# Three groups of blocks instead of two in a fused RWKV layer with routed experts

## The chip, the cores and the metric

The kernel runs on one core of one Trainium2 chip. The metric is the device time of one execution in microseconds; less is better. The core has five engines, each with its own queue of instructions that it works through in order: TensorE (PE in the profile, its weight loads PEld), VectorE (DVE), ScalarE (ACT), GpSimd (POOL) and SyncE (SP, which here only issues DMAs). They meet through semaphores. DMAs are issued from SP, from ACT at the start, and from GpSimd where the addresses come from data.

## The reference

The input is `x`, 8 sequences of 1024 tokens with 256 features, all float32. Two layers follow each other, each with a residual:

```
x = x + rwkv(layernorm(x))           # time mix, then channel mix, each with its own layernorm inside
x = x + experts(layernorm(x))

# time mix: r, w, k, v = projections 256 -> 256
e = exp(w + k), w = -exp(...)
num = decay * num + e * v ; den = decay * den + e     # along the 1024 tokens
x = x + Wo(sigmoid(r) * num / den)
# channel mix: 256 -> 1024 -> 256
x = x + sigmoid(Wrec xn) * Wval(relu(Wkey xn) ** 2)

# experts, 32 of them, 256 -> 128 -> 256
gates = sigmoid(xt @ expert_sel.T)
sel_val, sel_idx = top_k(gates, 4)
out = sum over the 4 chosen e of sel_val_e * relu(xt @ keys[e]) @ values[e]
```

The 8192 tokens make 32,768 pairs of token and expert.

## The kernel before

**Blocks.** The tokens are cut into 16 blocks of 512 (`TB`). `period(i)` (L943) emits in one pass the dense work of several blocks that are at different places: the channel mix of block `i` (`channel`, eight slices of 128 of the 1024 inner features), the time mix of block `i + 1` (`mix_wk`, `mix_vr`, `mix_scan`, `mix_out`), the first norms of block `i + 2`, and the routing of block `i - 1` (`norm_d` to `gates_by_row`). `total_blocks + 1` periods are emitted, and the last one holds only the routing of block 15. The result of the channel mix goes to DRAM as `acc` (`channel_end`, L424), the start value for the later sums.

**Scatter.** `gates_of` finds the four chosen experts of each token, and `rows_of` (L482) gives each pair a row in a DRAM buffer `xs` that has one region per expert. A region has place for all the tokens of a group and for one tile more. `scatter` (L527) queues 16 indirect DMAs per block, one for 128 tokens and one of the four choices; `post` (L543) issues them from GpSimd, two per `advance`. Each row carries its token's features and 8 tags, by which its place in the result is found again. `clear` (L170) fills the front of each region beforehand, so that rows which no token takes are told by their tag.

**Groups.** `GROUPS = (11, 5)`: blocks 0 to 10 are group 0, blocks 11 to 15 group 1. Each group has its own `xs`, and its own `ys` for the experts' results. When a group's blocks are all scattered, `tile_table` (L571) works out on VectorE, from the group's counts, which expert and which rows each tile of 256 (`TS`) rows has. A group has `tokens * 4 / 256 + 16` tiles, since the rows of an expert seldom fill a whole tile: 88 + 16 = 104 and 40 + 16 = 56. The last 16 tiles of a group have two halves with different experts.

**Experts.** `experts(g, pause)` (L687) is a generator that emits one step per tile. A step fetches a tile two steps ahead (`fetch`, SP), transposes one (`turn`, TensorE; `trx`), copies the key weights of its expert (`keys`, VectorE, 315 ns a copy), multiplies an earlier one with the keys (`hidden`; `ph`), and a still earlier one with the values (`result`; `po`, L800). ACT copies the result to `yg` (L865), and `send` (L810) issues two indirect DMAs from GpSimd that write the rows to their places in `ys` (L812); rows without a token have a place out of bounds and are not written. `places` (L740) works out these places as `to`. There are three `yg` buffers and six `to` buffers, and each comes free when the sends that read it have landed.

**Sums.** `combine(g)` (L869) is a generator too. A part of it has 128 tokens: a load of their four result rows each (`g`, 512 KB, L887) and four additions on VectorE (`ac`, L894), each a multiplication by the gate and an addition. Four parts make a block, whose start value is loaded from `acc` and whose sum is stored to `out`. A load from `ys` has to wait until all sends of the group have landed. Group 0 has 44 parts, group 1 has 20.

**What sets the order.** The list `background` holds generators with a rate. `advance` (L919), of which a period has 16, posts two scatters and lets each generator take as many steps as its rate says. `beside` adds a generator, and `drain` advances until the list is empty. The order of emission is:

```
    for i in range(total_blocks + 1):
        if i == len(groups[0]) + 1:
            post(len(waiting))
            beside(experts(0, 4), 113 / (STEPS * 3))
        if i == total_blocks - 1:
            drain()
            beside(combine(0), 0.5)
        period(i)
        ...
    post(len(waiting))
    beside(experts(1, 0), 1)
    drain()
    beside(combine(1), 1)
    drain()
```

So group 0's tiles lie in periods 12 to 14, its sums begin in period 15 and go on beside group 1's tiles, and group 1's sums stand alone at the end. A scheduler then orders the instructions of each engine; the tiles keep their order (`pinned`).

Of the kernel before, what the change touches and what calls it, by code (L numbers as in the profile page):

```python
# [8 lines left out]
F32 = mybir.dt.float32  # L9
# [4 lines left out]
ALU = mybir.AluOpType  # L14
# [5 lines left out]
P = 128  # L20
# [5 lines left out]
NOWHERE = float(1 << 20)  # L26
RUN = 8
TS = 256
GROUPS = (11, 5)


@with_exitstack
def rwkv_then_routed_experts(
# [18 lines left out]
    nc = tc.nc  # L52
    B, S, D = x.shape
    F = w_key.shape[-1]
    NE = w_exp.shape[1]
# [78 lines left out]
    region1, xs, ys, n_tiles, regions = [], [], [], [], []  # L134
    for g, members in enumerate(groups):
        gt = len(members) * TB
        r = const.tile([P, NT, NE], F32, name=f"region1_{g}")
        nc.gpsimd.iota(
            r,
            pattern=[[0, NT], [gt + TS, NE]],  # L140
            base=TS + 1,
            channel_multiplier=0,
            allow_small_or_imprecise_dtypes=True,
        )
# [24 lines left out]

    def clear(g):  # L170

        zeros = p3.tile([P, DX], F32, tag="k2", name=f"zeros_{g}")
        nc.gpsimd.memset(zeros, 0.0)
        nc.gpsimd.memset(zeros[:, D : D + 1], NOWHERE)
        front_rows = xs[g][: regions[g], :].rearrange("(e r) d -> e r d", e=NE)[:, :TS, :]
        fills = []
        for j in range(SJ):
            fills.append(
                nc.sync.dma_start(
                    out=front_rows[:, j * P : (j + 1) * P, :].rearrange("e p d -> p e d"),  # L180
                    in_=zeros[:, None, :].to_broadcast([P, NE, DX]),
                )
            )
# [118 lines left out]
    def mix_scan(i, c):  # L302
        n = blocks[i][1]
        m = mine[i]
        ek, ev, rc, tail = m["ek", c], m["ev", c], m["rw"][:, c, :], m["tail"]
        last = mine[i - 1]["tail"] if n else None
        num0 = last[:, 0, c : c + 1] if n else 0.0
        den0 = last[:, 1, c : c + 1] if n else 0.0
        decay = edec[:, c : c + 1].to_broadcast([P, TB])
        nc.vector.tensor_tensor_scan(ek, decay, ek, den0, ALU.mult, ALU.add)  # L310
        nc.vector.tensor_tensor_scan(ev, decay, ev, num0, ALU.mult, ALU.add)
        if n + 1 < NB:
            nc.gpsimd.tensor_copy(tail[:, 0, c : c + 1], ev[:, TB - 1 : TB])
# [168 lines left out]
    def rows_of(i):  # L482
# [18 lines left out]
            nc.tensor.matmul(ps, ones, prior, start=False, stop=True, skip_group_check=True)  # L501

        key = p2.tile([P, NT, NE], F32, tag="key", name=f"key_{i}")
        nc.vector.tensor_tensor(key, ps, region1[g], ALU.add)
        nc.vector.tensor_tensor(key, key, chosen, ALU.mult)
        k8 = p2.tile([P, NT, 8], F32, tag="k8", name=f"k8_{i}")
        for t in range(NT):
# [50 lines left out]
    def gates_by_row(i):  # L558
# [9 lines left out]
            nc.vector.tensor_reduce(gate[:, :, k], eq, AX.X, ALU.add)  # L568
        routed[i] = gate

    def tile_table(g):  # L571


# [23 lines left out]
        up = small([NE], "up", I32)  # L597
        nc.vector.tensor_scalar(up, ps, float(H - 1), None, ALU.add)
        base = small([NE], "base")
        nc.vector.tensor_tensor(base, ps, region1[g][:, 0, :], ALU.add)  # L600
# [42 lines left out]
        for k in range(3):  # L643
# [21 lines left out]
        nc.vector.scalar_tensor_tensor(  # L665
            say, whole, live[:, 0:1], say, ALU.mult, ALU.add
        )


        stride = len(groups[g]) * TB + TS  # L670
# [9 lines left out]
        nc.tensor.transpose(ps, say.rearrange("p a b -> p (a b)"), ident)  # L680
        table = keep.tile([4, P], I32, name=f"table_{g}")
        nc.vector.tensor_copy(table, ps)
        return table, limit

    WHY = "made from counts that sum to the group's choices"

    def experts(g, pause):  # L687

        table, limit = tile_table(g)
        T = n_tiles[g]  # L690
        yield

        EXPERT, ROW = range(0, 4, 2)
        most = {EXPERT: NE - 1, ROW: regions[g]}
# [140 lines left out]
        for step in range(-FETCH, T + 2 * STAGE):  # L835
# [16 lines left out]
            if step < T:  # L852
                xgT = turned[step] = p3.tile([P, KC, TS], F32, tag="xgT", name=f"xgT_{g}_{step}")

                move = nc.scalar.copy if g == len(groups) - 1 else nc.vector.tensor_copy
                after(move(xgT, trx), signal)  # L856
                to[step] = places(step, xg)
            if step < T:
# [73 lines left out]
    def drain():  # L932
        while background:
            advance()

    def beside(stream, rate):
        background.append([stream, rate, 0.0])

    def do(piece, i, *args):
# [77 lines left out]
    mix_vr(1, 1)  # L1017
    apply_c(0)
    mix_scan(1, 0)
    for i in range(total_blocks + 1):  # L1020
        if i == len(groups[0]) + 1:
            post(len(waiting))
            beside(experts(0, 4), 113 / (STEPS * 3))
        if i == total_blocks - 1:
            drain()
            beside(combine(0), 0.5)
        period(i)
        if i == 0:
            clear(1)
        if 1 <= i < 5:  # L1030
            load_experts(i - 1)
    post(len(waiting))
    beside(experts(1, 0), 1)
    drain()
    beside(combine(1), 1)
    drain()


# [42 lines left out]
```

## Time and profile before

| | us |
|---|---|
| median of the runs (3) | 1632.53 |
| lowest and highest | 1628.62, 1640.68 |
| the profiled execution, its time | 1447.24 |
| its span | 1445.5 |

The profiled execution is quicker than the runs. Its mean granted TensorE clock was 0.948 of full speed. The page gives for its engines:

| engine | busy us | share |
|---|---|---|
| PE | 1253.0 | 87% |
| PEld | 883.6 | 61% |
| DVE | 982.9 | 68% |
| ACT | 554.6 | 38% |
| POOL | 646.2 | 45% |

In the profile, a line such as `L812 POOL DMA_INDIRECT ys<-yg,to` names the source line, the engine, the operation, and what is written from what. In a timeline the first two numbers are the start and the duration in us; what stands in brackets at the end is the time that the engine was idle before and what ended it ("issue" means that nothing which the profile shows was waited for). A row of a table of windows has the window, its length, busy time and number of instructions for PE, PEld, DVE, ACT and POOL, then the mean granted clock of TensorE, the share of time that the DMA engines were busy, and GB/s. For DMAs issued by GpSimd, the duration on POOL is not the time to landing.

### The profile page before, as it was taken

How to read it: one execution, taken by the hardware profiler on the slowest of the kernel's cores; microseconds unless marked ns; L12 is line 12 of the kernel's file. 1: busy time of each engine (PE TensorE's matmuls, PEld its weight loads, DVE VectorE, ACT ScalarE, POOL GpSimd, SP SyncE). 2: the span in 40 equal slices, each digit the busy share in tenths (PEclk: the TensorE clock that was granted, in tenths of full speed). 3: DMA queues.
4: the chain of work that ended last, by engine and by line, in shares of the span. 5: the costliest groups of instructions: out<-in, count | busy, mean ns of one | idle time of the engine just before them, and what ended most of it. 6: DMA issues, size and time to landing. Idle time of an engine off the chain costs nothing. (4 is left out here: it accounts for less than half of the span.)

```text
span 1445.5 us, 18879 instructions
## 1 busy us (share of the span) xinstructions
PE 1253.0 (87%) x5332; PEld 883.6 (61%) x5332; DVE 982.9 (68%) x3336; ACT 554.6 (38%) x1066; POOL 646.2 (45%) x653
## 2 busy tenths in 40 slices
PE   5899999999999999999889999999998752888730
PEld 2566666666566666666568767877787531666630
DVE  5757787787797797797758656765675375464528
ACT  3343543543543533534423443344332420444410
POOL 2112352351441441442436765776577344667640
PEclk9999999999999999999999999999999875999975
DMA  9244331421210210211234654555443486989748
GB/s 325 69 158 129 137 109 47 140 98 58 83 68 30 82 64 34 82 60 38 92 117 135 191 165 132 156 182 170 129 155 113 140 292 199 292 317 304 246 167 298
DMA packets 119415, 209.75 MB, mean 145 GB/s; under 512 B 17137, under 2 KB 77570, under 8 KB 118800
## 3 DMA queue, kind: packets, MB, share of 16 engines
q1 hardware_dynamic: 89616, 138.71, 31.1%
q0 software_dynamic: 27648, 68.23, 12.7%
q10 hardware_dynamic: 2048, 1.61, 0.3%
q8 instruction: 44, 0.72, 0.2%
q14 instruction: 59, 0.48, 0.1%
HBM read 105.68 MB, written 111.17 MB: 150 GB/s over the span
## 5 line engine op out<-in xcount | busy, mean ns | idle before, releaser
L812 POOL DMA_INDIRECT ys<-yg,to x320 | 324.3, 1013 | 212.2 <-ACT yg L865 129.4
L548 POOL DMA_INDIRECT xs<-x,row x256 | 254.7, 995 | 318.4 <-issue 291.6
L242 PE MATMUL pj_f<-xT,wkey 128*128 128x512 f32 x512 | 242.6, 596 | 0.0
L410 PE MATMUL cm<-wval,k 128*128 128x256 f32 x1024 | 240.0, 379 | 0.0
L410 PEld LDWEIGHTS cm<-wval,k 128*128 128x128 f32 x1024 | 194.3, 190 | 73.2 <-issue 52.1
L784 PE MATMUL ph<-xgT,key 128*128 128x256 f32 (+1 forms) x768 | 172.7, 355 | 37.3 <-DVE key L763 24.1
L402 ACT ACTIVATE k<-pj_f 128x512 f32<-128x512 f32 x128 | 76.4, 597 | 251.7 <-PE pj_f L242 251.7
L784 PEld LDWEIGHTS ph<-xgT,key 128*128 128x128 f32 x768 | 131.5, 195 | 64.8 <-issue 38.8
L800 PE MATMUL po<-wexp,hs 128*128 x640 | 167.8, 386 | 0.6 <-issue 0.6
L894 DVE SCALAR_TENSOR_TENSOR ac<-g,gate,ac 128x256 f32<-128x256 f32 x256 | 120.3, 482 | 68.9 <-DMA g<-ys 64.9
L862 ACT ACTIVATE hs<-ph 128x256 f32<-128x256 f32 x160 | 61.7, 386 | 193.9 <-PE trx L772 186.8
L242 PEld LDWEIGHTS pj_f<-xT,wkey 128*128 128x128 f32 x512 | 92.6, 190 | 65.1 <-issue 61.7
L856 DVE COPY xgT<-trx 128x512 f32<-128x512 f32 x104 | 71.0, 682 | 83.5 <-PE trx L772 83.3
L772 PE MATMUL trx<-ident,xg 128*128 128x128 f32 x640 | 100.0, 280 | 29.1 <-DMA xg<-xs 28.5
L800 PEld LDWEIGHTS po<-wexp,hs 128*128 128x128 f32 x640 | 113.8, 194 | 16.4 <-issue 6.2
L772 PEld LDWEIGHTS trx<-ident,xg 128*128 128x128 f32 x640 | 79.9, 144 | 47.5 <-DMA xg<-xs 17.3
L318 DVE RECIPROCAL rw<-rw 128x512 f32<-128x512 f32 x32 | 106.6, 3332 | 0.6
L865 ACT COPY yg<-po 128x512 f32<-128x512 f32 x160 | 93.5, 584 | 20.8 <-DMA ys<-yg,to 20.6
L403 ACT ACTIVATE k<-k 128x512 f32<-128x512 f32 x128 | 80.6, 630 | 4.0
L754 DVE TENSOR_TENSOR to<-order,xg 128x2 uint32<-128x2 f32 x160 | 25.9, 162 | 77.0 <-DMA ys<-yg,to 74.0
L856 ACT COPY xgT<-trx 128x512 f32<-128x512 f32 x56 | 32.8, 585 | 113.6 <-PE trx L772 112.8
L297 DVE TENSOR_TENSOR ev<-pj_v,ek 128x512 f32<-128x512 f32 x32 | 22.1, 691 | 75.9 <-PE pj_v L242 75.0
(173 smaller groups left out, 1827.4 us busy)
## 6 DMA issues: line engine op xcount, KB each, us to landing
xg<-xs SPq DMA_DIRECT2D x128, 264.0 KB, 3.0
g<-ys SPq DMA_DIRECT2D x64, 512.0 KB, 5.4
xs<-zeros SPq DMA_DIRECT2D x4, 4224.0 KB, 17.1
xg<-xs SPq DMA_DIRECT2D x64, 132.0 KB, 2.5
x<-in_x SPq DMA_DIRECT2D x16, 512.0 KB, 3.8
acc<-x SPq DMA_DIRECT2D x16, 512.0 KB, 2.9
wexp<-in_w_exp SPq DMA_DIRECT2D x4, 2048.0 KB, 11.0
ac<-acc SPq DMA_DIRECT2D x16, 512.0 KB, 5.5
```

The lines of the kernel that those rows point to most:

```text
L242: nc.tensor.matmul(ps, w(c), rhs[:, c, :], start=(c == 0), stop=(c == KC - 1))
L318: nc.vector.reciprocal(rc, rc)
L403: nc.scalar.activation(k2, k2, AF.Square)
L410: nc.tensor.matmul(m["cm"][t // 2][:, t % 2, :], k2[:, t * P : (t + 1) * P], wval[:, f, :], start=(f == 0 and t % 2 == 0), stop=(f == FC - 1),
L548: s = nc.gpsimd.indirect_dma_start(out=xs[g], out_offset=bass.IndirectOffsetOnAxis(ap=m["row"][:, t, k : k + 1], axis=0), in_=m["x3"][:, t ...
L772: nc.tensor.transpose(ps[:, c, j * P : (j + 1) * P], xg[:, j, c * P : (c + 1) * P], ident)
L784: nc.tensor.matmul(ps[:, cols], key[:, c * P : (c + 1) * P], xgT[:, c, cols], start=(c == 0), stop=(c == KC - 1),)
L800: nc.tensor.matmul(ps[:, j, :], hs[:, j * P : (j + 1) * P], wexp[:, bass.ds(e, 1), KC * P :], start=True, stop=True,)
L812: s = nc.gpsimd.indirect_dma_start(out=ys[g], out_offset=bass.IndirectOffsetOnAxis(ap=to[:, j : j + 1], axis=0), in_=yg[:, j, :], in_offse ...
L856: after(move(xgT, trx), signal)
L865: after(nc.scalar.copy(yg, po), signal)
L894: nc.vector.scalar_tensor_tensor(ac, gk, routed[i][:, t, k : k + 1], ac, ALU.mult, ALU.add)
```

## The change

`GROUPS` becomes (10, 5, 1): blocks 0 to 9, 10 to 14, and block 15 alone. The groups have 80 + 16 = 96, 40 + 16 = 56 and 8 + 16 = 24 tiles, 176 in all instead of 160, and 40, 20 and 4 parts of sums.

- Group 0's tiles start one period earlier, in period 11, and its sums in period 14.
- Group 1's tiles start in period 16, beside the routing of block 15.
- `tile_table` becomes a generator with one `yield`, behind the work on VectorE and ahead of the matmuls that turn the table round. `beside` takes the first step of a generator at once, so the first half is emitted then. `run` lets some steps pass between the halves (6 for group 0, 4 for group 1); for group 2 two advances lie between.
- Group 1's sums get the rate 0.7 and are put beside group 2's tiles (rate 1). Group 2's four parts stand alone at the end, with the more numerous load buffers that the last group had before.
- Group 1 and group 2 both let ACT copy the transposed tiles.
- `region1` no longer holds four equal copies, and the addition reads it by a broadcast. `clear` takes its zeros from another pool, and is called for the three groups in a row. The experts' weights are loaded one block later.

```
-GROUPS = (11, 5)
+GROUPS = (10, 5, 1)
...
-        r = const.tile([P, NT, NE], F32, name=f"region1_{g}")
+        r = const.tile([P, NE], F32, name=f"region1_{g}")
...
-        zeros = p3.tile([P, DX], F32, tag="k2", name=f"zeros_{g}")
+        zeros = p2.tile([P, DX], F32, tag="g", name=f"zeros_{g}")
...
-        nc.vector.tensor_tensor(key, ps, region1[g], ALU.add)
+        nc.vector.tensor_tensor(key, ps, region1[g][:, None, :].to_broadcast([P, NT, NE]), ALU.add)
...
     def tile_table(g):
...
+        yield
         stride = len(groups[g]) * TB + TS
...
-        return table, limit
+        tables[g] = table, limit
...
     def experts(g, pause):
-        table, limit = tile_table(g)
+        table, limit = tables[g]
         T = n_tiles[g]
-        yield
...
-                move = nc.scalar.copy if g == len(groups) - 1 else nc.vector.tensor_copy
+                move = nc.scalar.copy if g else nc.vector.tensor_copy
...
     def beside(stream, rate):
+        next(stream)
         background.append([stream, rate, 0.0])
...
+    def run(g, wait, pause):
+        making = tile_table(g)
+        next(making)
+        for _ in range(wait):
+            yield
+        for _ in making:
+            pass
+        yield from experts(g, pause)
+
     for i in range(total_blocks + 1):
-        if i == len(groups[0]) + 1:
+        if i == groups[0][-1] + 2:
             post(len(waiting))
-            beside(experts(0, 4), 113 / (STEPS * 3))
-        if i == total_blocks - 1:
+            beside(run(0, 6, 4), (n_tiles[0] + 9) / (STEPS * 3))
+        if i == groups[0][-1] + 5:
             drain()
             beside(combine(0), 0.5)
+        if i == groups[1][-1] + 2:
+            post(len(waiting))
+            beside(run(1, 4, 0), 1.6)
         period(i)
-        if i == 0:
-            clear(1)
-        if 1 <= i < 5:
-            load_experts(i - 1)
+        if i < 2:
+            clear(i + 1)
+        elif i < 6:
+            load_experts(i - 2)
     post(len(waiting))
-    beside(experts(1, 0), 1)
+    making = tile_table(2)
+    next(making)
+    for _ in range(2):
+        advance()
+    for _ in making:
+        pass
     drain()
-    beside(combine(1), 1)
+    beside(combine(1), 0.7)
+    beside(experts(2, 0), 1)
+    drain()
+    beside(combine(2), 1)
     drain()
```

More of the change, by code (lines that the diff above doesn't have):

```diff
@@ L136, in rwkv_then_routed_experts @@
         gt = len(members) * TB
-        r = const.tile([P, NT, NE], F32, name=f"region1_{g}")
+        r = const.tile([P, NE], F32, name=f"region1_{g}")
         nc.gpsimd.iota(
             r,
-            pattern=[[0, NT], [gt + TS, NE]],
+            pattern=[[gt + TS, NE]],
             base=TS + 1,
@@ L569, in gates_by_row @@
         routed[i] = gate
+    tables = {}
     def tile_table(g):
@@ L599, in tile_table @@
         base = small([NE], "base")
-        nc.vector.tensor_tensor(base, ps, region1[g][:, 0, :], ALU.add)
+        nc.vector.tensor_tensor(base, ps, region1[g], ALU.add)
         fh_i = small([2, NE], "fhi", I32)
```

## The prediction

> **What bounds the kernel now.** I read the slices of the page first, then windows, the timeline around the stage borders, and the chain. All times are of the profiled execution, 1447.2 us (span 1445.5 us plus 1.7 us around it).
>
> From the page, the slices (36 us each):
>
> ```profile
> PE   5899999999999999999889999999998752888730
> ...
> POOL 2112352351441441442436765776577344667640
> PEclk9999999999999999999999999999999875999975
> ```
>
> TensorE is full until about 1110 us, dips, and is not full again. GpSimd fills up exactly where tiles run.
>
> Windows of engine time (PE, weight loads, DVE, ACT, POOL with counts; then clock, DMA share, GB/s): a plain block; three blocks beside group 0's tiles; from the last block's store to the first send of group 1; the tiles of group 1; the end.
>
> ```profile
> 647.00:702.00 55.00, 54.13 (x205) 34.87 (x205) 43.48 (x146) 24.20 (x45) 21.11 (x22) 1.00 0.17 60
> 702.00:1095.00 393.00, 373.53 (x1794) 291.55 (x1795) 253.12 (x922) 151.19 (x315) 239.52 (x238) 0.98 0.49 150
> 1176.00:1232.00 56.00, 17.25 (x80) 13.52 (x81) 34.04 (x161) 7.69 (x16) 20.21 (x21) 0.57 0.69 227
> 1232.00:1380.00 148.00, 118.80 (x654) 96.32 (x652) 77.78 (x310) 68.71 (x150) 103.22 (x101) 0.99 0.87 287
> 1398.00:1446.00 48.00, 0.00 (x0) 0.00 (x0) 35.94 (x80) 0.00 (x0) 0.28 (x1) 0.50 0.82 297
> ```
>
> The first two rows are TensorE-bound. In the third TensorE works 17 of 56 us, in the last not at all. The fourth looks unsaturated on every engine, but the timeline of GpSimd shows that a send of 0.98 us is followed by 0.30 us without another reason:
>
> ```profile
> 1215.55 0.96 POOL L548 DMA_INDIRECT xs<-x,row  x1 [0.30 <-issue]
> 1231.74 1.11 POOL L812 DMA_INDIRECT ys<-yg,to  x1 [15.23 <-ACT yg L865]
> ...
> 1380.03 0.98 POOL L812 DMA_INDIRECT ys<-yg,to  x1 [0.30 <-issue]
> ...
> 1397.29 0.98 POOL L812 DMA_INDIRECT ys<-yg,to  x1 [0.30 <-issue]
> ```
>
> So a send cannot come faster than every 1.29 us, two per tile, 2.58 us. Over the 104 intervals from 1231.74 to 1380.03 one took 1.426 us: GpSimd is 90% taken, and the rest is waiting for `yg`. The chain's largest item is the same place, the landing of a send that frees a `yg` or `to` buffer:
>
> ```profile
> DMA ys<-yg,to 5%; DVE ac L894 2%; POOL ys L812 2%; DMA g<-ys 2%; DVE key L763 0%; DMA xg<-xs 0%; DVE to L754 0%; PE ph L784 0%; DVE order L752 0%; POOL xs L548 0%; DVE later L744 0%; DVEq L703 0%; POOLq L1077 0%; POOLq L812 0%; PE trx L772 0%
> ```
>
> TensorE's timeline gives its price of a tile beside blocks, and the stall of the table:
>
> ```profile
> 705.63 0.18 PE L596 MATMUL count<-total,ones 128*128 128x32 bf16 x1
> 711.68 0.39 PE L675 MATMUL all<-scratch,ones 128*128 128x256 bf16 x1 [5.87 <-DVE scratch L674]
> ...
> 764.25 1.03 PE L800 MATMUL po<-wexp,hs 128*128 x4
> 765.11 1.03 PE L784 MATMUL ph<-xgT,key 128*128 128x256 f32 x4
> 765.98 0.60 PE L772 MATMUL trx<-ident,xg 128*128 128x128 f32 x4
> 766.41 1.03 PE L800 MATMUL po<-wexp,hs 128*128 x4
> ```
>
> One tile is 766.41 - 764.25 = 2.16 us of TensorE.
>
> **What the Trainium skill says.** *Perfetto Trace Analysis*, DMA Instruction - SWDGE: for a DMA issued by GpSimd the profiled end is the end of descriptor generation, not of the movement. The trace agrees: a send shows 1013 ns, yet the chain holds a separate "DMA ys" item after it. *DMA: Bandwidth & Descriptors*, Anatomy of one DMA: about 2 us of such a DMA are fixed, mostly the write receipt. The trace's shortest is 2.4 us (last send 1397.29, next load 1399.71), and up to 6.8 us when DMA is busy. *TensorE: Matmul & The Clock Gate*, What's actually happening: after a few idle microseconds TensorE drops to half clock. The trace agrees: 0.50 in the last window. The same page, Architectural detail, says that ACT and DVE are strict first-in first-out; so a sum waiting for its load holds the tile operations behind it.
>
> **The change, part by part** (instructions counted in the order in which the changed program issues them).
>
> (a) *Fewer tiles beside blocks.* Group 0 has 80 + 16 = 96 tiles, not 104. 8 x 2.16 = -17.3 us, all TensorE-bound. The table's first half is now several advances ahead of its matmuls, so the 5.87 us stall goes: -5.9 us; bounds -5.9 and 0; what is late next there is nothing, TensorE has block work queued. But 13 tiles, not 10, are left after the last block's matmuls; uncovered they go at 2.74 us (10 in the 27.4 us from 1094.9 to 1122.3): 3 x 0.58 = +1.7. Sum -21.5.
>
> (b) *Sums beside block 14.* 10 parts of sums enter a block period. DVE there has 43.5 of 55 us taken; 10 parts x 4 additions x about 0.44 us (39 in 17.27 us at the end of the trace) = 18 us, less the 6 us of norms that no block 16 needs: 55 us, just TensorE's time. The period after it has DVE work of about 20 + 11 x 1.76 = 39 us against 35 of TensorE. +1, bounds 0 and +6. The 8 us in which TensorE waits behind ACT's `yg` copies at the end of group 0 (1122.3 to 1130.3) only move from block 15 to block 14.
>
> (c) *The gap before group 1.* From the store of the last block (1176.1) to the first send are 55.6 us: norms, gates, 16 scatters of block 15, then table and first tile. Group 1 now needs block 14, whose scatters end 5 us after that store (1181.1 against 1176.1). The first fetch came 1.6 us after the last scatter, the first send 13.6 us after that fetch: 20.2. The table needs 7.5 us of DVE after the store, with a few sums between; On SP one load of sums stands ahead of that fetch, and its buffer is free by then. I take 24, bounds 20 and 30. -31.6.
>
> (d) *The send stage.* It grows from 112 sends to 160 (56 + 24 tiles) plus the 16 scatters of block 15, now in the same queue of GpSimd, ahead of sends 8 to 18 of group 1; who waits for that is `yg`, then ACT, then TensorE. 159 intervals x 1.426 = 226.7; 16 x 1.27 (scatter and gap) = 20.3; where scatters stand GpSimd does not idle, -(24 x 0.136) = -3.3. Where group 2 takes over, SP has the load of g for block 10 ahead of group 2's sixth fetch, and it can go only when all of group 1 has landed; the tiles already fetched cover most of it: +5, bounds 0 and +12. 248.7 us against 165.6 (1231.74 to 1397.29): +83.1. The interval itself is the largest unknown: floor 1.29; ceiling the old stage's mean with its end, 165.6 / 111 = 1.49.
>
> (e) *The end.* From the last send's start to the end are 48.2 us: 20 parts. Now 4 parts are left: landing 2.4, load 3.3 (1399.71 to 1403.04), 16 x 0.44 = 7.1, last store 3.0: 15.8. The sums of blocks 10 to 14 lie beside group 2's tiles; five parts are issued after the last fetch, some 16 us, and the sends still queued then cover about 27 us. -32.4; bounds -33 and -24.
>
> (f) *At nothing.* Clearing a third region writes another 8.7 MB near 60 us, with DMA 9% busy at 40 to 80 us; without that cover about 25 us of DMA. The smaller region1 and its broadcast: 16 additions of 283 ns stay what they are. Group 2's second table half stands on TensorE among tiles; its `limit` waits for group 1's last tile and keeps one PSUM bank meanwhile; ACT frees the others within a tile. Experts' weights load one block later, long before use.
>
> Sum: -21.5 + 1 - 31.6 + 83.1 - 32.4 = -1.4 us, 1445.8 on the profile's own time. The runs' median, 1632.53, is 12.8% above it; nothing shown says why. I assume that TensorE-bound stretches are longer there, so the 17.3 us become 19.5: -3.6, **1629 us**.
>
> **The rivals.** *No waiting for buffers.* Scatters and fewer sums per tile (19 parts beside group 1, not 26) keep GpSimd full: interval 1.31, handover 2: 159 x 1.31 + 20.3 + 2 = 230.6, 18 us less: **1611**. For it: beside group 0 sends run back to back at 1.29. Against: DMA was 87% busy beside group 1, and landings free the buffers.
>
> *Sums ahead of tiles.* DVE and SP take sums and tiles in one order; next to group 2 sums come at 0.7 per tile, not 0.5, and each that waits for its load holds up a tile. Interval 1.49, no filling of idle slots, handover 12: 236.9 + 20.3 + 12 = 269.2, 20.5 us more: **1650**. It decides from a mean of (248.7 + 19.9) / 175 = 1.535 us per interval; then the kernel is over 1% slower. For it: additions waited 64.9 us for loads in the trace. Against: most of that is the end, which shrinks.
>
> That the parts don't overlap at all can be excluded: the issue order has them mixed.
>
> **How the numbers follow.** 1% (16 us) is about what a measurement of this kernel can tell from no change. Forecast, within 1%: 0.48. First rival: 0.30, since it needs only that known idle slots fill. Second: 0.22. The range takes in both centres with some of the bounds of (b) and (c): 1606 to 1652. Chances: faster 0.30, same 0.48, slower 0.22.
>
> **What would show it.** The last block's store at about 1154 us (not 1176) shows (a) and (b); the first send of group 1 about 24 us after it shows (c); 175 intervals of GpSimd in about 249 us show (d); the end 16 us after the last send shows (e). No 5.87 us wait before the table's matmul. I am wrong if the interval is far from 1.43 us, or if the runs' unexplained 185 us lie in the send stage, which this change lengthens, rather than in the blocks.

## The result

The kernel after takes 1645.8 us (median of 20 runs), the kernel before, in the same series, 1633.7 us (20 runs, 1627.5 to 1643.2). The ratio is 1.0055, 95% interval 1.0038 to 1.0073: 0.55% slower. One of the 20 runs of the kernel after was slow (1747.7 us, at a granted clock of 0.804 where the others had 0.907 to 0.915) and is left out of the ratio. The medians by themselves differ by 12.1 us, 0.74%. I had forecast 0.2% faster, 1629 us. The time lies in my range, but the sign is wrong, and the difference is larger than the measurement is uncertain. The profiled execution of the kernel after took 1644.6 us (span 1642.9), so here the profile stands for the runs. That of before, 1447.2, did not.

The slices of the page after (41 us each; tenths busy, and tenths of full clock granted):

```profile
PE   6999987979879779797988988998687675677772
POOL 2114134043042241321566566556614436655563
PEclk9999988989889899898999989999898987898896
```

Before, TensorE was at 9 or 8 up to 1110 us. Here the row drops to 7 or 8 every few slices from about 200 us on, in blocks without tiles, whose work the change leaves as it was, and the clock drops with it. The windows of engine time say it in figures (PE, weight loads, DVE, ACT, POOL with counts; clock, DMA share, GB/s): a plain block; the periods beside group 0's tiles and sums; last block's store to first send; group 1's sends; group 2's; the end.

```profile
412.40:479.00 66.60, 57.27 (x205) 35.79 (x205) 43.83 (x145) 24.31 (x43) 18.95 (x18) 0.91 0.23 81
744.80:1256.50 511.70, 451.78 (x2037) 337.54 (x2037) 308.91 (x1108) 178.45 (x364) 268.49 (x267) 0.94 0.43 131
1307.00:1333.00 26.00, 11.44 (x54) 9.45 (x54) 15.46 (x97) 7.09 (x15) 3.79 (x4) 0.61 0.62 202
1333.00:1539.00 206.00, 142.87 (x732) 118.39 (x731) 81.49 (x389) 72.83 (x162) 126.14 (x127) 0.87 0.65 206
1546.00:1625.00 79.00, 54.63 (x309) 46.58 (x308) 50.98 (x170) 28.18 (x63) 48.47 (x47) 0.89 0.81 256
1625.00:1643.00 18.00, 0.00 (x0) 0.00 (x0) 7.40 (x16) 0.00 (x0) 0.99 (x1) 0.50 0.53 183
```

A plain block took 55.0 us with 54.1 of TensorE in the profile before; now it takes 66.6 with 57.3. For the same work there are now nine microseconds in which TensorE's record is empty, and three more in which it is busy. So most of the 197 us between the two profiles (the medians differ by 12) are not the change, and the two cannot be subtracted. What can be read from this one are the stage borders. The timeline of GpSimd (start, duration, in brackets the idle time before it and what ended it):

```profile
1333.26 1.00 POOL L815 DMA_INDIRECT ys<-yg,to  x1 [21.56 <-ACT yg L868]
...
1539.22 0.99 POOL L815 DMA_INDIRECT ys<-yg,to  x1 [0.30 <-issue]
1546.01 1.23 POOL L815 DMA_INDIRECT ys<-yg,to  x1 [5.80 <-ACT yg L868]
...
1625.19 0.99 POOL L815 DMA_INDIRECT ys<-yg,to  x1 [0.30 <-issue]
```

The last block's store is issued at 1307.1 us. First send 26.2 us later (I said 24), end 17.7 us after the last send (I said 15.8). The sends take 291.9 us, and I had said 248.7: 206.0 us for group 1's 111 intervals (1.86 each), 6.8 for the handover, 79.2 for group 2's 47 (1.69). The wait of 5.87 us for the first table is gone; TensorE's timeline has its matmul in the middle of block work, with no wait:

```profile
762.68 0.81 PE L385 MATMUL rec<-att,xT 128*128 128x256 f32 x3
763.32 0.27 PE L679 MATMUL all<-scratch,ones 128*128 128x256 bf16 x1
763.43 0.27 PE L684 MATMUL tr_say<-ident,scratch 128*4 128x128 f32 x1
```

### What the block is waiting for

The timeline of the same profile at one of these places:

```profile
406.37 1.96 PE L236 MATMUL tr_b<-ident,xn 128*128 128x128 f32 x8
...
410.70 0.69 DVE L431 SCALAR_TENSOR_TENSOR sg<-sg,cm 128x512 f32<-128x512 f32 x1 [2.83 <-remote]
...
414.96 0.78 ACT L275 ACTIVATE xT<-tr_b,csb 128x512 f32<-128x512 f32 x1 [7.44 <-remote]
...
415.79 2.08 PE L243 MATMUL pj_w<-xT,att 128*128 128x512 f32 x2 [7.45 <-ACT xT L275]
417.82 0.78 ACT L275 ACTIVATE xT<-tr_b,csb 128x512 f32<-128x512 f32 x1 [2.09 <-remote]
```

TensorE's last transpose is recorded as over at 408.3 us, but the copy that needs it starts at 414.96. "Remote" means that the view finds no instruction whose recorded end fits the semaphore's time. The copy waits for the transposes and VectorE's product for matmuls recorded before them, so what comes late is TensorE's own signal. TensorE looks as if it waited for ACT, and ACT as if it waited for nobody. The windows around it:

```profile
400.00:408.30 8.30, 7.99 (x34) 5.36 (x32) 6.50 (x31) 3.57 (x8) 6.16 (x8) 1.00 0.27 98
408.30:412.30 4.00, 0.04 (x1) 0.00 (x0) 1.59 (x4) 0.00 (x0) 3.08 (x4) 1.00 0.31 115
412.30:415.80 3.50, 0.01 (x1) 0.01 (x1) 2.96 (x17) 0.78 (x1) 2.78 (x3) 0.50 0.92 258
415.80:422.50 6.70, 5.91 (x7) 2.27 (x8) 0.00 (x0) 3.34 (x6) 0.00 (x0) 0.50 0.83 329
422.50:430.00 7.50, 7.50 (x30) 4.76 (x30) 5.04 (x11) 4.22 (x8) 0.00 (x0) 1.00 0.00 1
```

By the records TensorE first stands still, with the full clock still granted for 4 us; the half clock follows and lasts 6.7 us into the next matmuls. The Trainium skill has the second half of this (*TensorE: Matmul & The Clock Gate*, What's actually happening): after an idle window TensorE falls to half clock. That it does so here, 4 us after the last recorded transpose, speaks for a real standstill, but does not prove one. The profile models the ends of matmuls, and the signals came one after another: the product got its own by 410.70 us, the first copy by 414.96, and the second copy of the same transposes only by 417.82, 2 us after the record has TensorE in the next product. TensorE may as well have worked slowly in this time. What causes it is in no record. I call such a stretch a stop, and a TensorE that has them braked. The profile before has no wait for "remote" at all.

### The profile page after: what moved, and what is told of

The parts are those of the page before. It is cut to its first block, busy times and chain, and to the rows that moved or that the text cites. A ratio compares the mean times of both kernels' runs of the same rounds, so it can differ in the third digit from the quotient of the medians.

```text
span 1642.9 us, 19910 instructions
## 1 busy us (share of the span) xinstructions
PE 1352.2 (82%) x5590; PEld 946.9 (58%) x5590; DVE 994.8 (61%) x3452; ACT 579.2 (35%) x1122; POOL 675.3 (41%) x688
## 4 chain that ended last, share of the span: by engine, by line
PE 44%; DVE 25%; another core or an unknown queue 9%; issue 8%; DMA 5%; ACT 4%; POOL 2%; SPq 0%; DVEq 0%; POOLq 0%; ACTq 0%
PE pj_f L243 7%; PE cm L411 5%; PE ph L787 5%; PE po L803 4%; PE pj_w L243 4%; PE pj_k L243 3%; DVE rw L319 3%; PE rec L385 3%; DMA g<-ys 3%; PE pj_v L243 3%; PE trx L775 3%; PE pj_r L243 2%; DVE ac L897 2%; DMA ys<-yg,to 2%
## 5 line engine op out<-in xcount | busy, mean ns | idle before, releaser
L815 POOL DMA_INDIRECT ys<-yg,to x352 | 354.0, 1006 | 283.2 <-ACT yg L868 176.9
L787 PE MATMUL ph<-xgT,key 128*128 128x256 f32 (+1 forms) x896 | 201.2, 360 | 45.1 <-DVE key L766 15.5
L803 PE MATMUL po<-wexp,hs 128*128 x704 | 195.6, 403 | 37.0 <-ACT hs L865 30.8
L787 PEld LDWEIGHTS ph<-xgT,key 128*128 128x128 f32 x896 | 157.1, 207 | 75.1 <-issue 40.8
L803 PEld LDWEIGHTS po<-wexp,hs 128*128 128x128 f32 x704 | 130.0, 202 | 60.3 <-ACT hs L865 33.0
L243 PE MATMUL pj_w<-xT,att 128*128 128x512 f32 x128 | 84.5, 787 | 84.5 <-ACT xT L275 70.5
L775 PE MATMUL trx<-ident,xg 128*128 128x128 f32 x704 | 115.1, 288 | 32.7 <-ACT xgT L859 16.8
L775 PEld LDWEIGHTS trx<-ident,xg 128*128 128x128 f32 x704 | 92.1, 150 | 53.7 <-ACT xgT L859 19.1
L859 ACT COPY xgT<-trx 128x512 f32<-128x512 f32 x80 | 47.0, 589 | 196.7 <-remote 64.6
L243 PEld LDWEIGHTS pj_w<-xT,att 128*128 128x128 f32 x128 | 27.8, 235 | 119.1 <-ACT xT L275 85.4
```

What stands on the lines that cost most here:

```text
L243: nc.tensor.matmul(ps, w(c), rhs[:, c, :], start=(c == 0), stop=(c == KC - 1))
L775: nc.tensor.transpose(ps[:, c, j * P : (j + 1) * P], xg[:, j, c * P : (c + 1) * P], ident)
L787: nc.tensor.matmul(ps[:, cols], key[:, c * P : (c + 1) * P], xgT[:, c, cols], start=(c == 0), stop=(c == KC - 1),)
L803: nc.tensor.matmul(ps[:, j, :], hs[:, j * P : (j + 1) * P], wexp[:, bass.ds(e, 1), KC * P :], start=True, stop=True,)
L815: s = nc.gpsimd.indirect_dma_start(out=ys[g], out_offset=bass.IndirectOffsetOnAxis(ap=to[:, j : j + 1], axis=0), in_=yg[:, j, :], in_offse ...
```

## Experiments

The series fell on two conditions: in the first the kernel before took 1447 us, in the others 1623 to 1634 us. The record gives the same chip, number 13, for the unbraked series (e1 to e4) and for the first braked one behind it (e5 to e8), so the condition does not belong to the chip, as my expectation of e5 below took it to. Every ratio is within one series, and to the kernel before unless said otherwise; profiles are compared across series only where both are named.

### The kernel before, with and without stops

> The kernel before, profiled once more, to have its stages in the condition of its timed runs (1634 us; the profile shown before the prediction spans 1445.5 us). Theory A, a tile costs more than I thought: the blocks lengthen from 54.8 to about 65 us as in the profile after, the last block stores at about 1330, and the 111 intervals between group 1's sends lengthen from 1.49 us to about 1.85 (165.6 to 205 us), because the same TensorE stops fall into the sends; span about 1630. Theory B, the sums beside the tiles cost the change its gain: the intervals stay near 1.5 us (166 us), since they were 1.86 in the profile after only because combine(1) and the third group's tiles ran beside other work; then the last block has to store near 1370 for the same span.

> The kernel before once more, beside the next three. The first look at it (e1_before) ran on a chip where it takes 1447 us and its stages are those of the profile that I predicted from; the verdict on the change comes from a chip where it takes 1634 us. If these runs fall on a chip of the second kind: blocks of about 65 us, a last store at about 1320, 112 sends at about 1.85 us (205 us), 50 us behind them. If they fall on the first kind: 54.9, 1177, 1.49 us and 48.5 us again.

> The kernel before once more, for a second pair of stages beside the kernel after. With blocks of 55 us: last store 1176 to 1180, then 55.6, sends 166, end 48.3. With TensorE braked (blocks of 65 us): 1335 to 1345, 55.7, 182, 48.5. If the stages between the last store and the end differ from these by more than 5 us, the account by stages is not to be trusted.

e1_before: span 1450.1, blocks of 54.9 us, 1.498 us between sends. e5 and e9: spans 1630.2 and 1622.6, blocks of 65.8 and 65.3 (mean from the store of block 3 to that of block 10), 1.637 and 1.632 us between sends. The same line of the same kernel in the table of groups (busy us, mean ns, then idle time before it and what ended it), e1_before first:

```profile
L274 ACT ACTIVATE xT<-tr_b,csb 128x512 f32<-128x512 f32 x32 | 23.2, 775 | 6.1 <-PE tr_b L235 6.1
```

```profile
L274 ACT ACTIVATE xT<-tr_b,csb 128x512 f32<-128x512 f32 x32 | 24.4, 777 | 105.8 <-remote 82.8 <-PE pj_w L242 12.4 <-issue 7.4
```

The copy costs 775 and 777 ns: it has not become slower, TensorE's signals come late. Only TensorE's own records have grown, where the half clock is granted: 1255.2 us busy in e1, 1314.6 in e9. Between e1 and e9 the last store moves by 157.3 us (1179.9 to 1337.2), the gap by 0.1 (55.5, 55.6), the sends by 14.9 (166.3, 181.2), the end by 0.1 (48.5, 48.6). So of the time that my prediction could not explain (185 us there, 172.5 between these two profiles) nine tenths lie in the blocks, as I had assumed, and one tenth in the sends; nothing lies where TensorE has little or nothing to do. Theory B of the first expectation (intervals of 1.5 us in the runs) fell, A held in part: 1.63 us, not 1.85.

### The kernel after, stage by stage

e2 was meant to put group 1's sums behind group 2's tiles:

```
-    beside(combine(1), 0.7)
     beside(experts(2, 0), 1)
     drain()
+    beside(combine(1), 1)
+    drain()
```

> The kernel after with one piece undone: the sums of group 1 are no longer beside the tiles of group 2, they come after them. Theory A (the tiles alone set the pace): group 2's intervals stay near 1.69 us and some 35 us of sums are added behind them, 1675 us or more. Theory B (sums and tiles hold each other up): group 2's intervals fall to 1.45 us (48 x 0.24 = 11 us won), what is added is at most 35 us, 1645 to 1665 us. If the sums stood wholly in the way of the tiles, nothing is lost: 1646 us.

1.0023 (1.0010 to 1.0036), 1449.8 us. The edit did not do it: the scheduler put the loads of the sums between the fetches again, as SP's timeline shows.

```profile
1356.70 0.33 SPq L890 DMA_DIRECT2D g<-ys  x1
1357.88 1.42 SPq L740 DMA_DIRECT2D xg<-xs  x2
1360.63 0.33 SPq L890 DMA_DIRECT2D g<-ys  x1
```

Neither theory is tested by it, but it shows the kernel after, all but unchanged, without stops. The kernel after itself ran four times more:

> The kernel after, unchanged, with its stages. Where before takes 1447 us: my prediction's own sum was 1445.8 us of span (ratio 0.999); the profile e2_sums_after_tiles, whose order of work turned out to be nearly that of the kernel after, says 1446 of span and a ratio of 1.002, with the last block's store at 1153, first send of group 1 at 1175, last send at 1429. Where before takes 1634 us: 1.0055 again. If the change were worth the same at both, 1.0055 everywhere.

> The kernel after once more. Two series gave it 1.0055 and 1.0011 to the kernel before, both with TensorE braked. Theory: its gain (blocks) and its loss (sends) both grow with the braking and nearly cancel, so that the rest of 0 to 9 us moves from series to series: 1.001 to 1.006 braked, 1.001 to 1.003 unbraked. A ratio below 0.998 or above 1.008 would say that something else decides.

> The kernel after, to stand beside e13 and e15. Braked: last store 1295, 24.8, sends 289, 17.7, ratio to before 1.001 to 1.006. Unbraked: 1153, 22, 254, 17.6, ratio 1.000 to 1.003.

> The kernel after. Braked (before at 1620 to 1635 us): last store 1295, 25, sends 289 to 294, 17.6, ratio to before 1.001 to 1.006. Unbraked (before at 1447): last store 1153, 22, sends 254, 17.6, ratio 1.000 to 1.003, as in e2_sums_after_tiles.

1.0011 (0.9996 to 1.0027), 1.0027 (1.0010 to 1.0044), 1.0008 (0.9984 to 1.0031) and 1.0030 (1.0014 to 1.0047), all braked. With the first series' 1.0055 the kernel after is 0.1 to 0.55% slower, and in two of these five series the interval includes 1; the intervals of the first two don't meet.

Stages from the times of issue (last store of a block, first and last send, end of span); unbraked is the profile of before that I predicted from (1447.24 us) against e2 (1448.11), braked is e9 (1624.38) against e10 (1628.03). Each lies within 2 us of its kernel's median in that condition's series. e1 (1451.86) lies 4.6 us above, and its last store comes at 1179.9 us:

| stage | my step | predicted | unbraked | change | braked | change |
|---|---|---|---|---|---|---|
| to the last store | (a), (b) | -20.5 | 1176.1, 1152.7 | -23.4 | 1337.2, 1294.5 | -42.7 |
| gap | (c) | -31.6 | 55.6, 22.1 | -33.5 | 55.6, 24.8 | -30.8 |
| sends | (d) | +83.1 | 165.6, 254.0 | +88.4 | 181.2, 289.3 | +108.1 |
| end | (e) | -32.4 | 48.2, 17.6 | -30.6 | 48.6, 17.7 | -30.9 |
| sum | | -1.4 | 1445.5, 1446.4 | +0.9 | 1622.6, 1626.3 | +3.7 |

Of the braked pair, from the timelines of SP and GpSimd, the store of block 10, the last store and sends at the borders, e9 and then e10:

```profile
742.20 0.37 SPq L432 DMA_DIRECT2D acc<-x  x1
1337.18 0.37 SPq L432 DMA_DIRECT2D acc<-x  x1
1392.80 1.09 POOL L812 DMA_INDIRECT ys<-yg,to  x1 [15.20 <-ACT yg L865]
1574.00 0.98 POOL L812 DMA_INDIRECT ys<-yg,to  x1 [0.30 <-issue]
...
736.08 0.37 SPq L433 DMA_DIRECT2D acc<-x  x1
1294.45 0.37 SPq L433 DMA_DIRECT2D acc<-x  x1
1319.28 1.00 POOL L815 DMA_INDIRECT ys<-yg,to  x1 [20.28 <-ACT yg L868]
1608.63 0.98 POOL L815 DMA_INDIRECT ys<-yg,to  x1 [0.30 <-issue]
```

So 6.1 of the 42.7 us in the first row are gained up to the store of block 10, before any of the tiles.

### The table in two parts alone

The kernel before with `tile_table` split, `run`, and the buffers for `region1` and `zeros`; groups stay 11 and 5.

```
-            beside(experts(0, 4), 113 / (STEPS * 3))
+            beside(run(0, 6, 4), (n_tiles[0] + 9) / (STEPS * 3))
...
-    beside(experts(1, 0), 1)
+    making = tile_table(1)
+    next(making)
+    for _ in range(2):
+        advance()
+    for _ in making:
+        pass
+    beside(experts(1, 0), 1)
```

> The kernel before, groups 11 and 5, with the tables made in two parts and nothing else of the change (the small buffer edits for region1 and zeros come with it). My prediction put 5.9 us on the wait of TensorE for the first table that this takes away: ratio to before about 0.996. If other work now ends last at the same place, or the wait only moves, 1.000. The rival that the whole gain of the change lies in other parts is served by 1.000 as well.

0.9996 (0.9981 to 1.0011). From the store of block 10 to that of block 15 it took 526.8 us against 532.4 in e1_before, -5.6, and against 528.9 in the profile that I predicted from, -2.1; I had put 5.9 on it. In this profile the sends took 170.9 against 166.3 in e1, which gives most of it back. I can't say why; the whole is worth nothing measurable.

### Sixteen more tiles alone

```
-        n_tiles.append(gt * TOP // TS + NE // 2)
+        n_tiles.append(gt * TOP // TS + NE // 2 + 16 * g)
```

> The kernel before with 16 more tiles in group 1 (72 for 56), which hold no token: they are fetched, computed and sent, but every row of their sends is out of bounds and moves nothing. It is the price of the third group's 16 tiles by themselves. My prediction: 32 sends x 1.43 us = 45.6 us, ratio 1.028. Theory A (a send interval of about 1.85 us in the timed runs): 32 x 1.85 = 59 us, ratio 1.036. If sends without bytes are cheap and the interval is set by landings: under 40 us, ratio 1.024 or less.

1.0258 (1.0229 to 1.0287), 37.6 us: 1.17 us for each of the 32 sends, nearest to the third case. In the profile the 32 take 41.4 us, 1.29 each, and the 112 sends ahead of them 158.9 where e1 has 166.3. The 32 write nothing, and GpSimd's timeline has them without a break at its floor:

```profile
1394.56 0.99 POOL L812 DMA_INDIRECT ys<-yg,to  x1 [0.30 <-issue]
1395.85 0.99 POOL L812 DMA_INDIRECT ys<-yg,to  x1 [0.30 <-DVE order L752]
...
1435.99 0.99 POOL L812 DMA_INDIRECT ys<-yg,to  x1 [0.30 <-issue]
```

So without a write to land, TensorE, ACT and VectorE of this kernel keep up with 1.29 us per send. This ran unbraked.

### Buffers for the rows of a send

```
-    p6 = ctx.enter_context(tc.tile_pool(name="p6", bufs=6))
+    p6 = ctx.enter_context(tc.tile_pool(name="p6", bufs=12))
```

> The kernel after with twelve buffers for the rows that a send goes to (12 for 6), so that VectorE no longer waits for the landing of a send before it can write the next (74 us in 40 waits between 1180 and 1345 us of e2_sums_after_tiles). Rival No waiting for buffers: TensorE's waits for key and later in the same stretch go (up to 30 us of 165), the send interval falls from about 1.57 to 1.35-1.43 us, 160 sends are 20 to 30 us shorter: ratio to the kernel after 0.98 to 0.987. My theory (the landing is as late as the next stage is busy; TensorE, GpSimd and the DMA engines set the interval together): within 6 us of the kernel after.

1.0001 (0.9985 to 1.0017), 1.4 us under the kernel after of the same series: nothing. Waits beside group 1's tiles (us, times, longest), e6_after, then e7:

```profile
DVE to L757 <- DMA ys<-yg,to: 68.1, 30, 5.6
...
DVE key L766 <- PE ph L787: 1.6, 1, 1.6
```

```profile
DVE later L747 <- DMA xg<-xs: 33.7, 15, 7.0
DVE key L766 <- PE ph L787: 29.9, 17, 4.9
```

The 68.1 us of waiting for landings are gone from the list, and VectorE now waits 33.7 us for fetched tiles (6.0 in e6) and 29.9 us for TensorE to free a `key` buffer. The interval of group 1 is 1.839 us against 1.822. Other waits took the place of the first. "No waiting for buffers" falls as far as these buffers go, with TensorE braked; a fourth `yg` was not tried.

### The sums held back

`combine(1)` stands behind the tiles as in e2, and a semaphore now holds the loads of group 1's sums until TensorE is done with the last `po` of group 2 (`not_before`).

```
-                nc.sync.dma_start(out=sums[i], in_=acc_d[i].rearrange("(t p) d -> p t d", p=P))
+                load = nc.sync.dma_start(out=sums[i], in_=acc_d[i].rearrange("(t p) d -> p t d", p=P))
+                if g == 1:
+                    not_before(load, 2)
...
-            nc.sync.dma_start(out=g4, in_=rows)
+            load = nc.sync.dma_start(out=g4, in_=rows)
+            if g == 1:
+                not_before(load, 2)
...
-    beside(combine(1), 0.7)
     beside(experts(2, 0), 1)
+    drain()
+    beside(combine(1), 1)
```

> The kernel after with the loads of group 1's sums held by a semaphore until TensorE is done with group 2's last tile, so that the sums really come behind the tiles. Theory A (the tiles set the pace, the sums beside them are free): group 2's interval stays at 1.6 us, and the 20 parts of sums are added, 20 x 1.9 = 38 us: 1485 us where the kernel after takes 1448 (1680 where it takes 1646). Theory B (both hold each other up, Sums ahead of tiles): group 2's interval falls to 1.43 us, 8 us are won, and about 30 us are added: 1478 us (1670). If they stood fully in each other's way: no change.

1.0297 (1.0268 to 1.0326), 1673.1 us, 47 us over the kernel after of its series. Windows, group 2's sends and what follows:

```profile
1524.00:1601.00 77.00, 53.88 (x315) 47.20 (x313) 17.55 (x92) 28.70 (x65) 47.36 (x48) 0.92 0.38 115
1601.00:1675.00 74.00, 0.00 (x0) 0.00 (x0) 42.99 (x92) 0.00 (x0) 0.21 (x1) 0.50 0.69 230
```

In e6_after the first of these stages is:

```profile
1527.00:1609.00 82.00, 58.48 (x314) 49.97 (x312) 49.93 (x169) 28.81 (x64) 48.58 (x48) 0.85 0.81 260
```

Group 2's interval falls from 1.721 to 1.600 us, 5.7 us over 47 intervals, and the end grows from 17.7 to 74.2. Both theories had something: sums beside the tiles cost about 6 us, and here they keep 57 us from the end. The 6 us are uncertain, since in the braked profiles of the kernel after (the first one, e6, e10, e14, e16) this interval lies between 1.672 and 1.764 us. And with the DMA engines 38% busy and no sums the interval is still 1.60 us, not 1.29: neither crowded DMA engines nor sums alone are what holds these sends when TensorE is braked.

### Other cuts: 11, 4, 1 and 12, 3, 1

```
-GROUPS = (10, 5, 1)
+GROUPS = (11, 4, 1)
```

> The kernel after with GROUPS (11, 4, 1) for (10, 5, 1): 176 tiles again, but 8 of them go from the sends behind the last block to the three periods beside the blocks. A tile costs 2 x 1.56 = 3.1 us in the sends and 2.4 us beside blocks (braked: 3.6 and 2.6): 8 x 0.7 = 6 us won (braked 8 us), ratio to the kernel after 0.995. Rival: where the tiles stand makes no difference, since TensorE does the same work in both places: 1.000. Rival: the sums of group 0, 44 parts and one period later, fall into the sends of group 1 and slow them: 1.003 or more.

> The kernel after with GROUPS (12, 3, 1): another 8 tiles go beside the blocks (112 tiles in periods 13 to 15), and group 0's 48 parts of sums start in period 16 only, together with group 1's tiles. By the price of a tile another 6 us won, 0.990 to the kernel after; but 48 parts of sums now lie beside 40 tiles, 80 sends or 125 us, in which the sums alone need 48 x 1.9 = 91 us of VectorE: rival Sums ahead of tiles says that the interval rises to 1.7 us or more and the end moves out by 10 us or more, 1.003.

1.0140 (1.0102 to 1.0178) and 1.0416 (1.0377 to 1.0456): both slower, where the price of a tile had promised a gain. In e11 the blocks 11 to 15 take 587.2 us against 558.4 in e10, 28.8 us for 8 tiles more, 3.6 us each; the sends are 11.1 us shorter. How much of this is the rival of the later sums (1.003 or more to the kernel after, 1.012 measured by the medians) was not separated. In e12 sums of groups 0 and 1 lie beside group 2 (some 35 parts in that stage, of which 12 can be group 1's), and its interval is 2.80 us. Its waits there (us, times, longest), of the engines and then of SP's queue:

```profile
POOL ys L815 <- ACT yg L868: 83.9, 18, 11.6
...
PE trx L775 <- DMA xg<-xs: 49.2, 16, 5.8
```

```profile
SPq L890 <- DVE ac L897: 30.2, 17, 3.2
SPq L890 <- DVE order L755: 15.3, 7, 2.3
```

TensorE waits for fetches (L740), which stand on SP behind loads of sums (L890), and these wait for VectorE to free a buffer. So "Sums ahead of tiles" is a real mechanism, at this place and with this many sums; in the kernel after it is small.

### Less TensorE work in the sends

```
-                for c in range(KC):
+                for c in range(KC if g == 0 else 1):
...
-                            stop=(c == KC - 1),
+                            stop=(c == KC - 1 or g > 0),
```

> The kernel after, in which the first product of the tiles of groups 1 and 2 takes only one of its two chunks of 128 channels: half of the matmuls of ph are left out (2 of the 12 or so full matmuls of a tile by time, about 0.7 us of 3.1 us), all else stays, so the result of those tiles is another one. Theory TensorE sets the pace of the sends when braked: the intervals fall from 1.84 and 1.69 us to about 1.55 and 1.45 us, 160 sends are 30 to 45 us shorter, ratio to the kernel after about 0.977. Rival, what lies beside the tiles sets it (sums, scatters, landings, GpSimd): less than 10 us, ratio over 0.994. On an unbraked TensorE both expect little: 1.56 to about 1.50 us, 5 to 10 us.

1.0003 (0.9977 to 1.0029) against 1.0008 for e14, the kernel after in the same series. Windows of group 1 and 2, e13, then e14:

```profile
1325.00:1520.00 195.00, 125.91 (x580) 98.49 (x581) 79.39 (x381) 71.35 (x158) 121.63 (x121) 0.83 0.66 210
1525.00:1600.00 75.00, 50.67 (x242) 39.59 (x242) 45.84 (x158) 30.01 (x67) 45.37 (x45) 0.91 0.81 253
```

```profile
1325.00:1520.00 195.00, 145.49 (x704) 118.78 (x702) 77.16 (x370) 69.80 (x155) 119.08 (x119) 0.86 0.66 209
1530.00:1605.00 75.00, 59.75 (x327) 50.41 (x328) 45.53 (x160) 29.62 (x68) 41.75 (x41) 0.91 0.81 255
```

TensorE has 14% less to do beside group 1, and the interval goes from 1.852 to 1.833 us. Beside group 2 it has 10% less over the whole stage (e14's window begins 6 us ahead of its first send), 49.2 us for 54.4, and the interval goes from 1.672 to 1.584. The sends are 10.8 us shorter together, and the end 6.0 us longer. My theory that the amount of TensorE's work sets the pace, with 30 to 45 us to win, falls. Late signals stay: ACT's transposed copies wait 53.7 us for "remote" in 8 waits (65.5 us in 13 in e14), the longest 12.2 us.

### No third group

The kernel after with GROUPS (10, 6); group 1's tiles start behind the last block, only two regions are cleared, and the experts' weights are loaded at their old place, as before the change. Shown is the first line of the edit.

```
-GROUPS = (10, 5, 1)
+GROUPS = (10, 6)
```

> The kernel after with the third group undone: GROUPS (10, 6), group 1 starts behind the last block as in the kernel before, its sums stand alone, tables in two parts stay. 160 tiles instead of 176. By the stages: last store as in the kernel after (1295 braked, 1153 unbraked), gap 55.6, 128 sends at before's interval of 1.63 (208 us) or 1.50 (192 us), end 48.6 + 4 parts of sums (some 7 us): 1614 braked, 1456 unbraked, so a ratio to before of 0.995 braked and 1.007 unbraked. Theory: the third group pays only where TensorE is not braked, since its 16 tiles are TensorE work and what it covers is not. Rival: the third group is worth the same in both, ratio to the kernel after the same.

> The kernel after with the third group undone, GROUPS (10, 6), as in e15_no_third_group. Braked: 0.9986 to before once more (0.9975 to the kernel after), the sends 205 us and the gap and the end together 66 to 76 us longer than with a third group. Unbraked: gap 56 to 60, 128 sends x 1.50 = 192, end 58, last store 1153: 1461, ratio to before 1.010, to the kernel after 1.008. Rival, the third group's worth does not depend on braking: the same ratio to the kernel after in both.

0.9986 (0.9965 to 1.0007) and 0.9977 (0.9959 to 0.9996), 4.0 and 8.5 us under the kernel after in the same series. In e15 the stages are 1301.4, 59.8, 205.1 and 58.1 us; I had said 1295, 55.6, 208 and 56, and a ratio of 0.995. From the store of block 10 on, e15 takes 877.4 us and e14 896.0: with TensorE braked the third group costs 19 us more than it covers there. Up to that store e15 is 10.7 us behind (747.0 against 736.3), at the place of the clearing and of the weights, and so more than half of it is lost again; (10, 6) with the later loads was not run. The unbraked half of the theory could not be tried: no further series was unbraked. Of all versions this is the quickest, by 0.2% at best, and only the second of its two intervals excludes 1.

## Why the prediction was wrong

The predicted sum was -1.4 us on the profile, scaled to -3.6 on the runs. Unbraked, the profiles give +0.9. That is near, but in part by luck: (a), (b) and (c) together gained 4.8 us more than I said, and (d) and (e) lost 7.1 more. The runs of e2 were 0.23% slower, not faster. Braked, as the change was timed, the sum fails.

(a), *fewer tiles beside blocks*, and (b): -20.5 predicted, -23.4 unbraked (-27.2 against e1). The table's 5.9 us measured 2.1 to 5.6. The 8 tiles were mis-sized: from block 10's store to block 15's, e2 takes 502.6 us and e3, with the table split but 104 tiles, 526.8. That is 24.2 us or 3.0 us per tile, where I took TensorE's own 2.16 us. Braked it is 3.6 us (e11 against e10). Spread over all tiles, what these five blocks take beyond 54.9 us each gives an estimate of 2.4 us per tile in both (228.1 us for 96, 252.3 for 104), so some 5 of the 24.2 us come from something other than the number of tiles; what it is was not found. (b) was not measured apart.

(c), *the gap*: -33.5 and -30.8, right; (e), *the end*: -30.6 and -30.9, right.

(f), *at nothing*: not so. Unbraked a block before takes 54.8 to 54.9 us; in e2 the second and third take 56.9 and 56.1, together 3.4 us more. e3, which has only two regions to clear and loads the weights at the old place, does not show it. Braked, the same edit pays: the first wait of over 2 us for "remote" ends at 154 to 156 us in e5, e9, e15 and e17, which clear two regions and load the weights early, and at 213 to 217 us in all ten profiles with three regions and later loads, a block later. The third clearing or the later weights do this; they were not taken apart.

(d), *the send stage*, is the step that failed: its interval, 1.426 us, was too small, for two reasons. First, I miscounted. From 1231.74 to 1380.03 there are 101 intervals, not 104 (the row of windows that I showed has x101 for GpSimd there), so one took 1.468 us. With it my own terms make 159 x 1.468 + 20.3 - 4.3 + 5 = 254.4 us, +88.8 and not +83.1, and the whole sum +4.3 us and not -1.4: slower. Measured unbraked, the stage took 254.0 us. This agreement is luck in part: group 1 took 173.4 us where these terms give 179.0, and group 2's interval was 1.60 us, 75.2 us in place of 69.0.

Second, and larger, that profile was unbraked, and the runs were not. Braked, the stage changed by +108.1 in place of +83.1: group 1's 111 intervals +23.0, the handover 5.7, group 2's 47 intervals 79.4. Before itself has 1.63 us in the timed condition. With that, and 16 scatters x 1.29 = 20.6, group 1 should take 111 x 1.632 + 20.6 = 201.8 us, and it took 204.2; group 2 should take 47 x 1.632 = 76.7, and it took 79.4. So the terms were nearly the right ones, and one of them, the interval, was miscounted and read from an execution that was not like the runs. Of the 25.0 us by which (d) was off, the count is 5.7.

The same holds for the line under the sum. I saw that the runs were 185 us longer than the profile, placed these in TensorE-bound stretches, and then scaled only the gain, 17.3 to 19.5 us, and nothing in the sends, which I took not to be TensorE-bound. With the stops (d) went from +88.4 to +108.1, and the row of (a) and (b) from -23.4 to -42.7. Of these 19.3 us, 9.0 arise up to the store of block 10 (650.1 against 647.2 unbraked, 736.1 against 742.2 braked), where of the change only (f) lies; behind it the gain went from 26.3 to 36.6. Between the terms is left what was measured, +3.8 us by the medians of the e10 series. The first series' difference, 9 us by its ratio and 12.1 by its medians, is larger. Its profile has the last store 12.6 us later than e10, and before has no braked profile in that series: this remainder stays open.

The rivals: "Sums ahead of tiles" had 1650 us, close to the 1645.8 measured, but for another reason. Its sums cost about 6 us in e8, not 20. "No waiting for buffers" (1611) falls with e7, as far as that goes.

## What to carry to other kernels

If the profiled execution is 11% quicker than the runs, take no interval from it for the runs until a plain, unchanged stage has been seen at the runs' pace; a change that trades work in one stage for work in another is the difference of two large terms, and both have to be read there. Padding that comes with every group (16 tiles here) is paid in whole, so a further group has to cover more idle time than it costs at the pace of the runs: here, e14 against e15, 75 us of gap and end were covered and 88 us of sends added. An interval that is multiplied by many sends deserves a second count: three too many made 1.468 into 1.426, and over 159 of them that is 6.7 us. A line ending in "remote" on a kernel of one core points at a late signal (none in the five unbraked profiles, 40 and more in each braked one), and the engine to look at is the one that should have sent it.

## What the runs showed of the hardware

- TensorE's signals can come several us behind the recorded ends of its matmuls (waits of up to 12.8 us, in e6), in plain blocks about once per block: 66 us for what takes 55. A mean clock of 0.91 goes with it; in the stretch looked at, the half clock came 4 us after the last recorded matmul. The copies out of TensorE's results keep their duration (775 and 777 ns); only late signals ("remote") and TensorE's own records at half clock show it. Whether TensorE stands still or works slowly is open, and so is the cause.
- It holds for a series and then may be gone or come: 1447 us in one, 1623 to 1634 us in the others, for the same kernel, and both on chip 13.
- 14% less TensorE work beside group 1 left the interval of its sends the same to 1% (e13, TensorE braked).
- Sends whose rows are all out of bounds write nothing, and cost GpSimd the same 0.99 us and 0.30 us between them as the others (e4).
